# A layer's results turned by VectorE instead of TensorE, with row sums taken from the weighted product

## The chip, the cores and the metric

The kernel runs on one core of a Trainium2 chip. The metric is the device time of one execution in microseconds; lower is better. All data is float32. The engines are called PE (TensorE, the matrix engine), DVE (VectorE), ACT (ScalarE), POOL (GpSimd) and SP (SyncE, which here issues every DMA).

## What is computed

The input x has 4 batches of 128 channels and 64 x 64 = 4096 positions. Two layers follow one another:

```
# layer 0, on GroupNorm(x): q, k of 64 channels, v and gate of 128 (sigmoid)
attn = softmax(q^T k / 8);  x = x + Wp (gate * (v attn^T)) * sp + bp
# layer 1, on tokens t (4096 x 128): h = LayerNorm(t), q = h W
t = t + softmax(q q^T) h                  # same q on both sides: scores are symmetric
# feed-forward part: Wx = LayerNorm(t) W^T, batch norm over all tokens, then
y_s = sigmoid(Wx_s + y_(s-1) V^T)         # a scan over the 4096 tokens
t = t + y
```

## The kernel before

**Layers and blocks.** `fast()` does the work; `general()` is a fallback that runs only where a check of the denominators or of the scan fails. Each batch goes through `layer0` and `layer1`. Queries are taken in blocks of 512 (`QB`; `NB` = 8 blocks, `NQ` = 4 tiles of 128 in a block). All matrices on PE are float32, so a product of 512 columns is two PE instructions.

**Layer 0** (`attention`) walks 16 steps per block: two score products, one Exp over 1024 columns (L233), a running sum `acc` of the exponentials on DVE (L240) and the weighted products (L426) two steps later. `finish` of layer 0 multiplies by the gate, projects, and brings x and the projection from channels-by-tokens to tokens-by-channels with `move`: DVE turns 32 x 32 blocks into a tile `d` (L269), SP writes `d` to a scratch tensor `turn_d` in DRAM (L274), and four reads (L276) bring the blocks to the right partitions. It then keeps the tokens `t` in DRAM (`t_d`), writes the normed tokens `h` and moves a turned copy of `h` to `qt`.

**Layer 1** uses the symmetry: it takes query blocks in the order 6, 7, 5, 4, 3, 2, 1, 0 and for block n only the key blocks a = n, n-1, ..., 0. A step is half a key block: two score products (L695), the Exp (L701) and, two steps later, the `direct` products with `h` (L562). For a < n the exponentials are also turned: DVE turns 32 x 32 blocks into `dd` (L706), 16 SBUF-to-SBUF DMAs of 64 KB bring them into place in `tt` (L735), and some four steps later `reversed_products` (L575) adds block n's share to block a. `quarter` fills the diagonal block's second half from the first. Results gather in `oacc`, channels by tokens (L589, L591).

**The denominators** are sums of exponentials. The Exp instructions leave them with an accumulator output in `slots` (one Exp per 512 columns, each followed by a read of the accumulator); for the turned part DVE adds up `tt` (L580). `count` watches how many shares a block has.

**Finishing a block** (`finish` of layer 1). When a block has all its shares, small jobs join the queue `pending`: `tokens` (four PE turns of `oacc` into one PSUM bank, L631; scaling and residual, L633; LayerNorm), `result` (four PE turns of the new tokens `t1`, L644, a copy on ACT, a store to `t2_d`), two empty places, `turn` (four PE turns of the normed tokens `h2`, L653, a copy to `th`) and `inputs` (one product, L658, batch-norm statistics L659, a copy L662/L665 and a store). After each step of attention one job leaves `pending`. An empty place (`nothing`), or a step with `pending` empty, takes a job from `ahead` instead: the next batch's preparation (`prepare`), with query/key products (L354, emptied by L358, L362 and L366), values (L374, then L379, L383, L384) and gates (L389, then L390, L393).

**PSUM.** `ps_s` holds two score tiles of two banks, `ps_o` three banks for `o` and `ot`, and `ps_m` a single bank for everything else: the turns and products of `finish`, `queries` (L520) and the preparation.

**What sets the order.** The code above gives the order in which instructions are recorded. A scheduler then places them engine by engine, and each engine runs its own queue in order: an instruction that waits holds up all behind it on that engine. SP's queue is in order too.

**The end.** After the last block of the last batch (`b == B - 1 and n == 0`), whose key blocks are taken in the order 1, 0, the scan starts: 44 steps of two halves, which need the `inputs` of every block. t2 is read back from `t2_d` and y added to it before the output is stored.

Of the kernel before, what the change touches and what calls it, by code (L numbers as in the profile page):

```python
# [49 lines left out]
def conv_attn_hybrid_kernel(  # L50
# [17 lines left out]
    turn_d = [dram.tile([P, 4, NQ, 32], F32, name=f"turn{i}_d") for i in range(8)]  # L68
# [60 lines left out]
    def scales():  # L129

        nc.vector.tensor_mul(w_v, w_v, bc[:, 0, :])
        nc.vector.tensor_mul(w_p, w_p, bc[:, 2, :])

        nc.vector.tensor_scalar(par2, par[:, SG : BG + 1], 0.5, None, ALU.mult)
# [31 lines left out]
def fast(  # L166
# [13 lines left out]
    with ExitStack() as st:  # L180
# [82 lines left out]
        def move(blocks, dst):  # L263

            nonlocal n_moves
            d = work.tile([P, 4, NQ, 32], F32, tag="d", name="d", bufs=2)
            turned = nc.vector.transpose(d.rearrange("q a j i -> q j a i"), blocks)  # L269
            if n_moves == 0:  # L270
                tc.keep_in_program_order(turned)
            via = turn_d[n_moves % len(turn_d)]
            n_moves += 1
            nc.sync.dma_start(via, d)  # L274
            for a in range(4):
                nc.sync.dma_start(dst[bass.ts(a, 32)], via[:, a].rearrange("(p i) j k -> i p j k", p=4))  # L276
# [18 lines left out]
        def tiles(t):  # L295

            return [t[:, :, j, :] for j in range(NQ)]

# [112 lines left out]
        def layer0(b, gate, q, k, v, need):  # L411
# [20 lines left out]
            def finish(n, o, acc):  # L432
# [12 lines left out]
                sub = stat.tile([P, NQ, 4], F32, tag="sub", name="sub", bufs=2)  # L445

                def sums():


                    half, blocks = acc[:, 0, :], acc[:, 1, :]  # L450
                    nc.vector.tensor_tensor(half, half, blocks, ALU.add)
                    nc.vector.transpose(blocks, half)
                    nc.vector.tensor_reduce(
                        sub, blocks.rearrange("q (j f k) -> q j f k", j=NQ, f=4), AX.X, ALU.add
                    )
                    move(xb.rearrange("c (j f k) -> c j f k", j=NQ, f=4), t)

                def denominators():
                    m0, m1 = halves(quart, sub.rearrange("q j f -> q (j f)"))
                    tot = stat.tile([P, NQ, 4], F32, tag="tot", name="tot", bufs=2)  # L460
                    flat = tot.rearrange("q j f -> q (j f)")
                    nc.vector.tensor_copy(flat, m0)
                    nc.vector.tensor_tensor(flat, flat, m1, ALU.add)
                    nc.vector.tensor_tensor(
                        tot, tot,
                        own.rearrange("q (j f) -> q j f", j=1).to_broadcast([P, NQ, 4]), ALU.mult,
                    )
                    den = den_all[:, b * NT + n * NQ : b * NT + (n + 1) * NQ]
                    nc.vector.tensor_reduce(den, tot, AX.X, ALU.add)
                    nc.vector.reciprocal(rinv, den)  # L470

                def projection():
                    m0, m1 = halves(wt["ps"], og)
                    nc.scalar.copy(og, m1)
                    nc.vector.tensor_tensor(og, m0, og, ALU.add)
                    move(og.rearrange("c (j f k) -> c j f k", j=NQ, f=4), yt)

                def tokens():
                    for j in range(NQ):
                        nc.vector.scalar_tensor_tensor(  # L480
                            t[:, :, j, :], yt[:, :, j, :], rinv[:, j : j + 1], t[:, :, j, :],
                            ALU.mult, ALU.add,
                        )
                    nc.sync.dma_start(t_d[b, n], t)
                    layernorm(tiles(t), quarters(h[:, ts, :]))

                    move(
                        h[:, ts, :].rearrange("q j (p i) -> q j p i", p=4),
                        qt[:, cs].rearrange("c (p j k) -> c p j k", j=NQ, p=4),
                    )  # L490
                    done.add((b, n))
# [6 lines left out]
        def layer1(b, h, qt):  # L498
# [7 lines left out]

            slots = accp.tile([P, NT, NB + 1], F32, tag="slots", name="slots", bufs=2)
            nc.gpsimd.memset(slots[:, :, NB:], 0.0)
# [14 lines left out]
            def quarter(n, ps, e, before, slots):  # L523
# [14 lines left out]
                for half in range(2):  # L538
                    at = NQ * n + 2 + half
                    nc.scalar.activation(  # L540
                        e[:, half, hb:], ps[:, 0, bass.ts(half, hb)], AF.Exp, bias=shift,
                        accum_out=slots[:, at, n : n + 1],
                    )
                for half in range(2):
                    at = NQ * n + 2 + half
                    nc.scalar.activation(
                        e[:, half, :hb], ps[:, 1, bass.ts(half, hb)], AF.Identity,
                        accum_out=slots[:, at, NB : NB + 1],
                    )

            def order(n):


                return [1, 0] if b == B - 1 and n == 0 else list(range(n, -1, -1))
# [15 lines left out]
            def reversed_products():  # L570
# [3 lines left out]
                for j in range(NQ):  # L574
# [5 lines left out]
                nc.vector.tensor_reduce(  # L580
                    slots[:, bass.ts(n, NQ), a], t.rearrange("q p b k j -> q b p (k j)"),
                    AX.XY, ALU.add,
                )
                part(a, ot)
                count(n)

            def part(n, o):
                if n in begun:
                    nc.vector.tensor_tensor(oacc[:, n, :], oacc[:, n, :], o, ALU.add)  # L589
                else:  # L590
                    nc.vector.tensor_copy(oacc[:, n, :], o)  # L591
                begun.add(n)
                count(n)

            def count(n):


                parts[n] += 1
                if parts[n] == NB - (b == B - 1 and n == 0):
                    finish(n)  # L600

            def finish(n):
                cs = bass.ts(n, QB)
                rinv = stat.tile([P, NQ], F32, tag="rinv", name="rinv")
                t = work.tile([P, 4, NQ, 32], F32, tag="t", name="t1", bufs=2)
                if b == B - 1 and n == 0:
# [3 lines left out]
                    th, t2 = two[:, 0, :], two[:, 1, :]  # L610
# [3 lines left out]
                else:  # L614
# [3 lines left out]
                    t2 = None  # L618
# [5 lines left out]
                def tokens():  # L624
                    at = (B + b) * NT + n * NQ
                    den = den_all[:, at : at + NQ]
                    nc.vector.tensor_reduce(den, slots[:, bass.ts(n, NQ), :], AX.X, ALU.add)
                    nc.vector.reciprocal(rinv, den)
                    m = bank().rearrange("q (j c) -> q j c", j=NQ)
                    for j in range(NQ):  # L630
                        nc.tensor.transpose(m[:, j, :], oacc[:, n, bass.ts(j, P)], ident)  # L631
                    for j in range(NQ):
# [7 lines left out]
                def result():  # L640
                    nonlocal t2
                    m = bank()
                    for j in range(NQ):
                        nc.tensor.transpose(m[:, bass.ts(j, P)], t1[:, j, :], ident)  # L644
                    if t2 is None:
                        t2 = work.tile([P, QB], F32, tag="xb", name="t2")
                    nc.scalar.copy(t2, m)
                    nc.sync.dma_start(t2_d[b, :, cs], t2)

                def turn():  # L650
# [3 lines left out]
                    nc.scalar.copy(th, m)  # L654

                def inputs():
                    m = bank()
                    nc.tensor.matmul(m, lhsT=wt["f"], rhs=th, start=True, stop=True)  # L658
                    nc.vector.bn_stats(bn_st[:, b * NB + n, :], m)  # L659
                    m = m.rearrange("p (g i s) -> p i g s", i=L // 2, s=2)  # L660
                    if b == B - 1:
                        nc.vector.tensor_copy(wxs[:, :, b, bass.ts(n, GB), :], m)  # L662
                    else:
                        wx = work.tile([P, L // 2, GB, 2], F32, tag="wx", name="wx")
                        nc.vector.tensor_copy(wx, m)  # L665
                        nc.sync.dma_start(wxs_d[b, :, :, bass.ts(n, GB), :], wx)

                if b == B - 1 and n == 0:
                    pending.appendleft(tokens)
                    pending.extend([result, turn, inputs])  # L670
                elif b == B - 1 and n < 4:
                    pending.extend([tokens, result, turn, inputs])
                else:
                    pending.extend([tokens, result, nothing, nothing, turn, inputs])


            for n in [NB - 2, NB - 1] + list(range(NB - 3, -1, -1)):
# [4 lines left out]
                for a in order(n):  # L682
# [4 lines left out]
                    for i in range(2):  # L687
                        ps = ps_s.tile([P, 2, QB], F32, tag="s", name="ps")
                        e = ep.tile([P, 2, QB], F32, tag="e", name="e")
                        if a == n and i == 1:  # L690
                            quarter(n, ps, e, before, slots)
                        else:
                            for half in range(2):
# [4 lines left out]
                                )  # L698
                            for half in range(2):
                                at = NQ * a + 2 * i + half  # L700
                                nc.scalar.activation(  # L701
                                    e[:, half, :], ps[:, half, :], AF.Exp, bias=shift,
                                    accum_out=slots[:, at, n : n + 1],
                                )
# [19 lines left out]
                        if a > n and i == 1:  # L724
                            count(a)
# [571 lines left out]
```

## Time and profile before

The median of three runs is 3062.62 us (3060.75 to 3062.82). One profiled execution took 3064.04 us, with a span of 3062.2 us and a mean granted PE clock of 0.992.

| What | Busy us or count |
|---|---|
| ACT, Exp of layer 0, L233 x512 | 520.8 |
| ACT, Exp of layer 1, L701 x516, and its accumulator reads | 350.0 and 101.3 |
| DVE, running sum of layer 0, L240 x448 | 547.3 |
| DVE, turns of exponentials, L706 x444 | 287.1 |
| PE turns of `finish`, L631, L644, L653, each x124 in the main form | 19.9, 18.9, 21.1 |
| POOL, bias added to x, L443 x32 | 61.7 |
| DMA, `tt<-dd` | 1776 issues of 64 KB, 2.0 us to landing |
| DMA, moves: writes of 256 KB, reads of 64 KB | 96 and 3 x 128 issues, about 2.0 us to landing |

Busy time counts overlapping PE instructions by their union, so the duration of one says less than the distance from its start to the next one's. In a row of a group, the figures after the bar are the busy time, the mean duration of one in ns, and the engine's idle time just before with what ended it.

### The profile page before, as it was taken

The page shows a single profiled execution, that of the slowest core. Times are in us where ns is not written, and L with a number is a line of the kernel's source. Part 1 is how long each engine was busy: PE and PEld are TensorE (multiplying, and loading weights), DVE is VectorE, ACT ScalarE, POOL GpSimd, SP SyncE. Part 2 cuts the span into 40 slices and gives each one's busy share as a digit, 9 for nine tenths or more (in the row PEclk, how much of TensorE's full clock was granted, in tenths as well). Part 3 has the DMA queues.
Part 4 walks back from the last instruction along what each step waited for, and adds up shares of the span by engine and source line. Part 5 has one row for each costly group of instructions (what it writes and reads, how often), then busy time and mean ns, then how long its engine had stood idle before and what let it go on. Part 6 is the DMA issues. An engine that isn't in the chain of part 4 may idle for free.

```text
span 3062.2 us, 32664 instructions
## 1 busy us (share of the span) xinstructions
PE 3006.4 (98%) x10844; PEld 1382.7 (45%) x10844; DVE 1880.9 (61%) x3160; ACT 1151.9 (38%) x2147; POOL 149.0 (5%) x187
## 2 busy tenths in 40 slices
PE   8999999999999999999999999999999999999996
PEld 4444444444444444444444444444444444444443
DVE  6666665655666666555566666665566666455556
ACT  3443433333344443333344443333334444323334
POOL 0000000000000000000000000000000000000000
PEclk9999999999999999999999999999999999999998
DMA  1111143433111123333311113333321112543334
GB/s 42 38 56 56 49 112 87 99 89 97 48 56 56 47 80 94 92 97 91 82 47 61 42 49 110 89 96 95 93 59 57 41 50 93 138 102 93 100 104 166
DMA packets 233746, 241.16 MB, mean 79 GB/s; under 512 B 88544, under 2 KB 144352, under 8 KB 232544
## 3 DMA queue, kind: packets, MB, share of 16 engines
q1 hardware_dynamic: 233568, 238.97, 28.0%
q8 instruction: 89, 1.46, 0.2%
q14 instruction: 89, 0.73, 0.1%
HBM read 65.80 MB, written 56.62 MB: 40 GB/s over the span
## 4 chain that ended last, share of the span: by engine, by line
PE 95%; DVE 3%; issue 1%; ACT 1%; POOL 0%; DVEq 0%; POOLq 0%
PE o L426 29%; PE o L562 16%; PE ps L231 15%; PE ps L695 14%; PE ot L575 12%; PE m L260 1%; PE m L658 1%; PE mq L520 1%; PE ps L528 1%; PE mp L389 1%; PE mp L354 1%; PE mp L374 1%; DVE t2s L881 1%; DVE ps_r L854 1%; PE m L653 1%
## 5 line engine op out<-in xcount | busy, mean ns | idle before, releaser
L426 PE MATMUL o<-e,nxt 64*128 64x512 f32 x4096 | 966.2, 589 | 0.0
L233 ACT ACTIVATE e<-ps 128x1024 f32<-128x1024 f32 x512 | 520.8, 1023 | 685.2 <-PE ps L231 669.7
L240 DVE TENSOR_TENSOR acc<-acc,e 128x1024 f32<-128x1024 f32 x448 | 547.3, 1222 | 236.5 <-ACT e L233 220.8
L426 PEld LDWEIGHTS o<-e,nxt 64*128 64x128 f32 x4096 | 400.1, 187 | 483.0 <-issue 474.2
L701 ACT ACTIVATE e<-ps,shift 128x512 f32<-128x512 f32 x516 | 350.0, 683 | 675.0 <-PE ps L695 510.8
L562 PE MATMUL o<-e,h 128*128 128x512 f32 x1160 | 539.5, 592 | 0.0
L231 PE MATMUL ps<-nxt 64*128 64x512 f32 x2048 | 535.3, 596 | 1.2 <-DVE nxt L366 0.9
L695 PE MATMUL ps<-qt 128*128 128x512 f32 x1032 | 490.9, 595 | 2.9 <-ACT qt L521 2.7
L575 PE MATMUL ot<-tt,h 128*128 128x512 f32 x888 | 399.6, 593 | 0.2 <-DMA tt<-dd 0.2
L706 DVE STREAM_TRANSPOSE dd<-e 128x512 f32<-128x512 f32 x444 | 287.1, 687 | 85.9 <-ACT e L701 75.4
L562 PEld LDWEIGHTS o<-e,h 128*128 128x128 f32 x1160 | 218.2, 190 | 265.8 <-issue 261.2
L231 PEld LDWEIGHTS ps<-nxt 64*128 64x128 f32 x2048 | 194.2, 187 | 228.9 <-issue 151.3
L695 PEld LDWEIGHTS ps<-qt 128*128 128x128 f32 x1032 | 187.9, 190 | 213.5 <-issue 188.7
L575 PEld LDWEIGHTS ot<-tt,h 128*128 128x128 f32 x888 | 167.9, 190 | 210.4 <-issue 207.5
L580 DVE TENSOR_REDUCE slots<-tt 128x4 f32<-128x2048 f32 x111 | 250.8, 2259 | 9.3 <-DMA tt<-dd 8.9
L589 DVE TENSOR_TENSOR oacc<-oacc,ot 128x512 f32<-128x512 f32 x87 | 59.6, 685 | 188.3 <-PE ot L575 188.2
L138 POOL TENSOR_SCALAR rstd<-mv 128x4 f32<-128x4 f32 x64 | 14.5, 227 | 2349.7 <-DVE mv L287 2349.7
L701 ACT ACTIVATION_READ_ACCUMULATOR e<-ps,shift 128x1 f32 x516 | 101.3, 196 | 0.0
L443 POOL TENSOR_SCALAR xb<-xb,bpc 128x512 f32<-128x512 f32 x32 | 61.7, 1929 | 389.1 <-DMA xb<-in_x_dram 372.0
L480 DVE SCALAR_TENSOR_TENSOR t<-yt,rinv,t 128x128 f32<-128x128 f32 x128 | 36.5, 347 | 71.4 <-DMA yt<-turn_d 66.3
L139 POOL TENSOR_TENSOR rstd<-rstd,mhalf 128x4 f32<-128x4 f32 x64 | 66.4, 1037 | 5.3
L290 DVE TENSOR_SCALAR h<-t,mv,rstd 128x128 f32<-128x128 f32 x128 | 35.7, 342 | 47.1 <-POOL rstd L139 47.1
(161 smaller groups left out, 1667.3 us busy)
## 6 DMA issues: line engine op xcount, KB each, us to landing
tt<-dd SPq DMA_DIRECT2D x1776, 64.0 KB, 2.0
turn_d<-d SPq DMA_DIRECT2D x96, 256.0 KB, 2.0
t_d<-t SPq DMA_DIRECT2D x63, 256.0 KB, 2.0
xb<-in_x_dram SPq DMA_DIRECT2D x32, 256.0 KB, 2.9
t<-turn_d SPq DMA_DIRECT2D x128, 64.0 KB, 2.0
yt<-turn_d SPq DMA_DIRECT2D x128, 64.0 KB, 2.0
qt<-turn_d SPq DMA_DIRECT2D x128, 64.0 KB, 2.1
t<-t_d SPq DMA_DIRECT2D x32, 256.0 KB, 3.1
```

The costliest lines, as they stand in the source:

```text
L139: nc.gpsimd.tensor_tensor(dst, dst, mhalf[:, :n], ALU.pow)
L231: nc.tensor.matmul(ps[:, h, :], lhsT=lhsT, rhs=rhs, start=True, stop=True)
L233: nc.scalar.activation(e, ps, AF.Exp, scale=scale)
L240: nc.vector.tensor_tensor(acc, acc, e, ALU.add)
L426: nc.tensor.matmul(o[r], lhsT=v[rs, p + h * PAIRS, :], rhs=e[rs, h, :], start=(p == 0 and h == 0), stop=(p == PAIRS - 1 and h == 1),)
L443: nc.gpsimd.tensor_scalar(xb, xb, bpc, None, ALU.add)
L562: nc.tensor.matmul(o, lhsT=h[:, NQ * a + 2 * i + half, :], rhs=e[:, half, :], start=(a == order(n)[0] and i == 0 and half == 0), stop=(a = ...
L575: nc.tensor.matmul(ot, lhsT=h[:, NQ * n + j, :], rhs=t[:, :, j, :, :].rearrange("q p k j -> q k p j"), start=(j == 0), stop=(j == NQ - 1),)
L580: nc.vector.tensor_reduce(slots[:, bass.ts(n, NQ), a], t.rearrange("q p b k j -> q b p (k j)"), AX.XY, ALU.add,)
L695: nc.tensor.matmul(ps[:, half, :], lhsT=qt[:, bass.ts(at, P)], rhs=qt[:, bass.ts(n, QB)], start=True, stop=True,)
L701: nc.scalar.activation(e[:, half, :], ps[:, half, :], AF.Exp, bias=shift, accum_out=slots[:, at, n : n + 1],)
L706: nc.vector.transpose(d.rearrange("q f b k j -> q k b f j")[:, 2 * i + half], e[:, half, :].rearrange("q (b f j) -> q b f j", b=NQ, f=NQ),)
```

## The change

The change does four things.

1. **Row sums from the product.** After `h` has been moved to `qt`, POOL adds 1 to it. As the channels of a normed token sum to zero, the channel sum of the weighted product is then 128 times the denominator. `slots`, the accumulator outputs, the reduction of `tt` and `count` go; one Exp covers 1024 columns in layer 1 as well. The product now gives the attention output plus 1, so 1 is taken from the bias added to x (`bpc`), which a LayerNorm doesn't notice.
2. **The result turned by DVE.** `result` no longer uses PE and ACT: `turn_out` turns the tokens on DVE and writes them to `t2_d` with four scattered DMAs.
3. **Blocks 4 to 7 of layer 1 wholly without PE turns.** `finish_moved` brings `oacc` to tokens with a `move`, scales and norms, brings the normed tokens back with a second `move`, and stores the result with `turn_out`. Its jobs are spread over nine places.
4. **The move the other way round.** Where it wrote once and read four times, it now writes four times, each to its place in DRAM, and reads once. The tiles of tokens are laid out accordingly.

A block now counts as finished when its products are there, and the last block takes its key blocks as 0, 1.

```diff
+        def turn_out(blocks, dst):
             d = work.tile([P, 4, NQ, 32], F32, tag="d", name="d", bufs=2)
             turned = nc.vector.transpose(d.rearrange("q a j i -> q j a i"), blocks)
...
+            for f in range(4):
+                nc.sync.dma_start(
+                    dst.rearrange("(a i) m -> i a m", a=4)[:, :, bass.ts(f, P)],
+                    d[bass.ts(f, 32)].rearrange("i a j k -> i a (j k)"),
+                )
...
-            nc.sync.dma_start(via, d)
-            for a in range(4):
-                nc.sync.dma_start(dst[bass.ts(a, 32)], via[:, a].rearrange("(p i) j k -> i p j k", p=4))
+            turn_out(blocks, via)
+            nc.sync.dma_start(dst, via)
...
+                    hn = h[:, ts, :].rearrange("q j c -> q (j c)")
+                    nc.gpsimd.tensor_scalar(hn, hn, 1.0, None, ALU.add)
...
-                nc.vector.tensor_reduce(
-                    slots[:, bass.ts(n, NQ), a], t.rearrange("q p b k j -> q b p (k j)"),
-                    AX.XY, ALU.add,
-                )
...
+            def finish_moved(n):
...
+                def sums():
+                    ot = work.tile([P, 4, NQ, 32], F32, tag="og", name="otk")
+                    move(oacc[:, n, :].rearrange("c (j f k) -> c j f k", j=NQ, f=4), flat(ot))
+                def tokens():
+                    reciprocals(n, ot.rearrange("q p j i -> q j p i"), AX.XY, rinv)
...
+                    layernorm(tiles(t), tiles(h2))
+                    th = work.tile([P, QB], F32, tag="th", name="thm")
+                    move(h2.rearrange("q p j i -> q j p i"), th)
+                    turn_out(t.rearrange("q p j i -> q j p i"), t2_d[b, :, cs])
+                def inputs():
+                    recurrence_inputs(n, th, ps_m.tile([P, QB], F32, tag="m", name="mw"))
+                gap = [nothing] * 3
+                pending.extend([sums, *gap, tokens, *gap, inputs])
+
+            def reciprocals(n, o, axes, rinv):
+                at = (B + b) * NT + n * NQ
+                den = den_all[:, at : at + NQ]
+                nc.vector.tensor_reduce(den, o, axes, ALU.add)
+                nc.vector.tensor_scalar(den, den, 1.0 / C, None, ALU.mult)
+                nc.vector.reciprocal(rinv, den)
...
             def finish(n):
+                if n >= 4:
+                    return finish_moved(n)
...
                 def result():
-                    m = bank()
-                    for j in range(NQ):
-                        nc.tensor.transpose(m[:, bass.ts(j, P)], t1[:, j, :], ident)
-                    nc.scalar.copy(t2, m)
-                    nc.sync.dma_start(t2_d[b, :, cs], t2)
+                    turn_out(t1.rearrange("q j (p i) -> q j p i", p=4), t2_d[b, :, cs])
...
-                elif b == B - 1 and n < 4:
-                    pending.extend([tokens, result, turn, inputs])
+                elif b == B - 1 and n < 4:
+                    pending.extend([tokens, turn, inputs])
                 else:
-                    pending.extend([tokens, result, nothing, nothing, turn, inputs])
+                    pending.extend([tokens, nothing, nothing, nothing, turn, inputs])
...
-                            for half in range(2):
-                                nc.scalar.activation(
-                                    e[:, half, :], ps[:, half, :], AF.Exp, bias=shift,
-                                    accum_out=slots[:, at, n : n + 1],
-                                )
+                            nc.scalar.activation(e, ps, AF.Exp, bias=shift)
```

## The prediction

> **What bounds the kernel now.** I read the page first (busy times and the chain that ended last).
>
> ```profile
> PE 3006.4 (98%) x10844; PEld 1382.7 (45%) x10844; DVE 1880.9 (61%) x3160; ACT 1151.9 (38%) x2147; POOL 149.0 (5%) x187
> PE 95%; DVE 3%; issue 1%; ACT 1%; POOL 0%; DVEq 0%; POOLq 0%
> L580 DVE TENSOR_REDUCE slots<-tt 128x4 f32<-128x2048 f32 x111 | 250.8, 2259 | 9.3 <-DMA tt<-dd 8.9
> ```
>
> TensorE carries 95% of the chain. VectorE has 39% free, so the 250.8 us of its L580, which the change removes, are worth nothing by themselves. Next, who made TensorE wait (columns: total us, times, longest):
>
> ```profile
> PE ps L695 <- ACT qt L521: 2.7, 4, 0.7
> PE mp L354 <- DVE nxt L366: 2.5, 3, 0.8
> PE ot L575 <- DMA tt<-dd: 0.2, 1, 0.2
> ```
>
> So between the load at the head and the scan, the in-order TensorE queue is full: every instruction taken off it counts, and so does every wait put on it. What a turn costs there, from the groups by shape and the TensorE timeline:
>
> ```profile
> L644 PE MATMUL m<-ident,t1b 128*128 128x128 f32 x124 | 18.9, 275 | 0.0
> L631 PE MATMUL m<-ident,oacc 128*128 128x128 f32 x124 | 19.9, 275 | 0.0
> ...
> 2923.22 0.60 PE L644 MATMUL m<-ident,t1b 128*128 128x128 f32 x4
> 2923.66 1.03 PE L528 MATMUL ps<-qt 128*128 128x256 f32 x4
> ```
>
> A turn lasts 275 ns, but four of them give way to the next instruction after 2923.66 - 2923.22 = 0.44 us, or 0.11 us each. By starts, a 128x512 product (two instructions) takes 0.86 us. Then how long the one PSUM bank of `ps_m` stays taken by a query/key product (timelines of TensorE and VectorE):
>
> ```profile
> 537.10 1.02 PE L354 MATMUL mp<-nxt,w 128*128 128x512 f32 x2
> 537.96 1.88 PE L695 MATMUL ps<-qt 128*128 128x512 f32 x4
> ...
> 538.16 0.80 DVE L358 TENSOR_SCALAR nxt<-mp,par 64x512 f32<-64x512 f32 x1 [4.71 <-PE mp L354]
> 539.80 0.82 DVE L366 TENSOR_SCALAR nxt<-mp,par 64x512 f32<-64x512 f32 x1 [0.84 <-ACT nxt L362]
> ```
>
> TensorE is done at 537.96 and the bank is free at 540.62: 2.6 us, filled here by other products. Last, the DMA queue in block 7 and the end of layer 1:
>
> ```profile
> 518.70 22.05 SPq L735 DMA_DIRECT2D tt<-dd  x32
> 543.21 24.07 SPq L735 DMA_DIRECT2D tt<-dd  x32
> ...
> 2957.85 3.60 PE L562 MATMUL o<-e,h 128*128 128x512 f32 x8
> 2961.29 0.60 PE L644 MATMUL m<-ident,t1b 128*128 128x128 f32 x4
> 2963.55 0.66 PE L631 MATMUL ml<-ident,oacc 128*128 128x128 f32 x4 [1.66 <-DVE oacc L589]
> 2965.37 2.08 PE L658 MATMUL m<-th,w 128*128 128x512 f32 x2
> 2975.60 4.33 PE L831 MATMUL ps_r<-wxs,ident 128*128 128x256 f32 x12 [1.47 <-DVE wxs L662]
> ```
>
> SyncE needs 0.65 to 0.75 us for each `tt` issue, nearly without a pause: a second tight resource. At the end, 14.3 us pass from the last product (2961.29) to the scan (2975.60), and after the idle stretch the same product takes 2.08 us where it took 1.02 before.
>
> [...]
>
> **The change part by part.** *Turns off TensorE.* Each of the 16 finishes of blocks 4 to 7 loses 12 turns, each of the other 16 loses 4 (the result): 256 turns, 64 groups of 0.44 us. The two result groups at the end (blocks 1 and 0 of the last batch) lie beside a wait: 62 x 0.44 = **-27.3 us**.
>
> *Row sums.* Adding 1 to `h` lets the channel sum of the weighted product give the denominators. Away go L580, 516 accumulator reads (196 ns each) and half of the Exp instructions. VectorE gains some 250 us and ScalarE 130, but neither ends a wait of TensorE worth over 3 us: **0**. The added `h`+1 on GpSimd (some 1.93 us, as L443) is queued before the next `xb` and LayerNorm on an engine 5% busy: 0.
>
> *Moves.* A move was one write and four reads and is now four writes and one read: five issues either way, 0.43 us for a scattered one, 0.34 for a whole one. The wait for the landing stays. Layer 0: 0, at most 1 us later per block.
>
> *Added moves and VectorE turns.* A finish of blocks 4 to 7 now puts 16 transfers on SyncE where there were 3: 12 x 0.43 for scattered writes plus two reads and a landing wait less the old store, about 7 us, and three VectorE turns of 0.71 us. What is queued behind: the `tt` transfers, for which reversed products wait. I compared each pair's last landing with its product in the trace: 3 to 14 us to spare in batches 0 to 2, 0.2 at worst in the last, and 6 to 12 where the moves fall; the new order sets the reversed products up to 10 us later. Hidden: **0**, at most +6 in the last batch.
>
> *The order of TensorE's queue.* The scheduler placed the next batch's preparation (`ahead`) anew. I walked both built programs' TensorE order with 0.86 us per product and 0.11 per turn, and listed where a user of the `ps_m` bank follows the one before sooner than that one is emptied. In the kernel before, this gives three places of weight, 1.72 us after an L354 each; the trace has just these: 2.5 us in 3 times. The changed order has, in each of batches 0 to 2:
>
> ```
> 775 L636 mw<-thm x1
> 776 L725 ps<-qt x2
> 777 L385 mp x4
> 778 L725 ps<-qt x1
> 779 L365 mp<-nxt,w x2
> 780 L385 mp<-w,nxt x4
> 781 L577 ot<-tt,h x4
> ...
> 813 L400 mp<-nxt,w x3
> ...
> 853 L636 mw<-thm,w x1
> 854 L672 m<-ident,oacc x4
> ```
>
> (L365, L385, L400, L636 are the former L354, L374, L389, L658.) At 779 and 780 nothing stands between: two waits of 2.6 us. At 813 two waits for ScalarE, 0.78 (L390) + 0.2 = 1.0 us each. At 854 the wait for statistics and copy, 0.70 + 0.67 + 0.1 = 1.45. A like place in the next layer 0, 0.6. Sum 9.3 per batch, times 3 = **+27.9 us**; the last batch, without preparation, +0.6. Behind the waiting instruction stand all products, and nothing can catch up.
>
> *The clock.* Around 779 to 781 TensorE works 0.86 us in some 6, and at the end of the trace before, 1.66 us of idleness among short turns was enough to double the time of a product. If it halves here, [...] **+6** (0 to 9).
>
> *The end.* Block 0's denominators now come after its turns: a reduction of 0.69, two small operations of 0.2 and a VectorE turn of 0.65 join the chain, +1.7 for block 1 and again for block 0; but block 1 starts sooner. From the last product I work out 15.3 to 16.4 us against 14.3: **+1.5**.
>
> Sum: 3062.6 - 27.3 + 27.9 + 0.6 + 6 + 1.5 = **3071 us**.
>
> **The rivals.** (a) *Clean gain*: the bank's waits don't occur, because the queue is then behind for other reasons or the emptying is quicker: 3062.6 - 27.3 + 1.5 = 3037. For: the turns surely go. Against: the same walk named the three waits of the kernel before. (b) *Cancelled*: the clock doesn't dip (-6) and the gates' waits are hidden (-6): 3071 - 12 = 3059.[...] (c) *DMA queue bound*: on top of mine, SyncE's 7 us come through in part; where half of it does in the tight blocks 7 (4 of 16 finishes), 4 x 3.5 = 14: 3085. For: SyncE is near full in block 7. Against: the slack named above.
>
> **How the numbers follow.** My case 0.52 (3066 to 3076, four fifths of it slower by over 0.2%), (b) 0.23, (a) 0.12, (c) 0.13. Above 3068.7: 0.42 + 0.13 and a little of (b) = 0.58; within 0.2% (3056.5 to 3068.7): 0.29; faster 0.13. The range takes in (b) and (c) up to their middles, with the clock from 0 to 9: 3055 to 3084.
>
> **What would show it.** TensorE's waits should list `mp` L365 and L385 for VectorE L377 with about 5 us per batch, L400 for ScalarE with 2, `m` L672 for VectorE with 1.5 to 2, and 256 fewer TensorE instructions; the granted clock should dip three times, at the start of block 5. A wait list as short as before makes (a) right; long waits of `ot` L577 for `tt` make (c) right.

## The result

The changed kernel takes 3088.86 us (median of four runs, 3086.51 to 3091.43), against 3062.72 us before (median of four runs, one more than above): ratio 1.0085, 95% interval 1.0067 to 1.0102. It is 26.1 us slower. The forecast was 3071 us, slower by 8.3, with a range up to 3084: the direction was right, the time lies above the range.

### The profile page after: what moved, and what is told of

It is laid out like the page before. It is cut to its first block, busy times and chain, and to the rows that moved or that the text cites. A ratio compares the mean times of both kernels' runs of the same rounds, so it can differ in the third digit from the quotient of the medians.

```text
span 3087.9 us, 31588 instructions
## 1 busy us (share of the span) xinstructions
PE 2991.4 (97%) x10588; PEld 1365.9 (44%) x10588; DVE 1698.4 (55%) x3146; ACT 1022.5 (33%) x1133; POOL 222.5 (7%) x215
## 4 chain that ended last, share of the span: by engine, by line
PE 88%; SPq 5%; DVE 4%; DMA 1%; issue 1%; ACT 1%; POOL 0%; DVEq 0%
PE o L437 29%; PE ps L233 15%; PE o L564 14%; PE ps L725 12%; PE ot L577 11%; SPq L759 5%; PE m L262 1%; PE mq L529 1%; PE mp L365 1%; PE mp L385 1%; PE mp L400 1%; PE ps L537 1%; DVE t2s L905 1%; DVE ps_r L878 1%; DMA tt<-dd 1%
## 5 line engine op out<-in xcount | busy, mean ns | idle before, releaser
L729 ACT ACTIVATE e<-ps,shift 128x1024 f32<-128x1024 f32 x258 | 287.1, 1113 | 801.6 <-PE ps L725 435.8
L233 PE MATMUL ps<-nxt 64*128 64x512 f32 x2048 | 545.8, 595 | 2.0 <-DVE nxt L377 0.9
L725 PE MATMUL ps<-qt 128*128 128x512 f32 x1032 | 483.8, 594 | 2.7 <-ACT qt L530 2.7
L577 PE MATMUL ot<-tt,h 128*128 128x512 f32 x888 | 411.4, 607 | 11.0 <-DMA tt<-dd 7.0
L732 DVE STREAM_TRANSPOSE dd<-e 128x512 f32<-128x512 f32 x444 | 278.1, 679 | 148.5 <-DMA tt<-dd 93.8
L577 PEld LDWEIGHTS ot<-tt,h 128*128 128x128 f32 x888 | 171.5, 195 | 227.7 <-issue 222.8
L502 POOL TENSOR_SCALAR h<-h 128x512 f32<-128x512 f32 x32 | 72.3, 2260 | 63.7 <-DVE d L270 59.6
L588 DVE COPY oacc<-ot 128x512 f32<-128x512 f32 x24 | 16.6, 692 | 86.7 <-PE ot L577 86.6
```

The source lines that it names most:

```text
L233: nc.tensor.matmul(ps[:, h, :], lhsT=lhsT, rhs=rhs, start=True, stop=True)
L502: nc.gpsimd.tensor_scalar(hn, hn, 1.0, None, ALU.add)
L577: nc.tensor.matmul(ot, lhsT=h[:, NQ * n + j, :], rhs=t[:, :, j, :, :].rearrange("q p k j -> q k p j"), start=(j == 0), stop=(j == NQ - 1),)
L725: nc.tensor.matmul(ps[:, half, :], lhsT=qt[:, bass.ts(at, P)], rhs=qt[:, bass.ts(n, QB)], start=True, stop=True,)
L729: nc.scalar.activation(e, ps, AF.Exp, bias=shift)
L732: nc.vector.transpose(d.rearrange("q f b k j -> q k b f j")[:, 2 * i + half], e[:, half, :].rearrange("q (b f j) -> q b f j", b=NQ, f=NQ),)
```

## The profile after

The page of the changed kernel gives these busy times and this chain of work that ended last:

```profile
PE 2991.4 (97%) x10588; PEld 1365.9 (44%) x10588; DVE 1698.4 (55%) x3146; ACT 1022.5 (33%) x1133; POOL 222.5 (7%) x215
PE 88%; SPq 5%; DVE 4%; DMA 1%; issue 1%; ACT 1%; POOL 0%; DVEq 0%
```

The 256 instructions are gone from PE, and VectorE and ScalarE are relieved as the change meant it. But the chain, which before was PE for 95% and had no share of SyncE's queue (SPq), is PE for 88% and the queue for 5%. The list of who made TensorE wait (total us, times, longest) has the names:

```profile
PE mp L365 <- DVE nxt L377: 9.4, 5, 2.6
PE mp L385 <- DVE nxt L377: 7.7, 3, 2.6
PE ot L577 <- DMA tt<-dd: 7.0, 4, 3.0
PE ml L688 <- DVE last L298: 6.9, 1, 6.9
...
PE m L672 <- DVE wx L643: 5.1, 6, 1.4
PE mp L400 <- ACT nxt L401: 4.3, 5, 0.9
...
PE ot L577 <- issue: 4.0, 4, 2.5
```

The lines of `mp` and of `m` L672 are the waits for the `ps_m` bank that the forecast named, at its places; 2.5 us of them, ahead of three L365, were there before. The two lines of `ot` L577, 11.0 us together, are new: before, `ot` waited for `tt` 0.2 us once. Next comes the first place where the preparation's products stand together, at the start of block 5 in batch 0, first in TensorE's timeline and then in windows of 3.41 us (first the length, then PE's busy time; the third figure from the right is the granted clock):

```profile
558.77 1.12 PE L365 MATMUL mp<-nxt,w 128*128 128x512 f32 x2 [2.56 <-DVE nxt L377]
562.45 2.08 PE L385 MATMUL mp<-w,nxt 128*128 128x128 f32 x8 [2.56 <-DVE nxt L377]
564.32 5.39 PE L577 MATMUL ot<-tt,h 128*128 128x512 f32 x8
```

```profile
557.68:561.09 3.41, 1.12 (x2) 0.30 (x2) 1.62 (x2) 0.50 (x2) 0.00 (x0) 1.00 0.35 57
561.09:564.51 3.42, 2.06 (x9) 2.06 (x10) 0.82 (x1) 0.45 (x1) 0.00 (x0) 0.50 0.00 0
564.51:567.92 3.41, 3.41 (x6) 1.34 (x5) 3.35 (x6) 1.92 (x3) 0.00 (x0) 0.50 0.00 0
567.92:571.33 3.41, 3.41 (x10) 1.50 (x9) 1.62 (x4) 0.94 (x1) 0.00 (x0) 1.00 0.31 77
```

TensorE waits 2.56 us twice, and then the granted clock is 0.50 for 6.83 us: eight instructions of L577, begun at half clock, take 5.39 us. What such a stretch of half clock, a dip, costs is shown best by two places that are alike, behind the `inputs` of a moved block (one that `finish_moved` finishes) in batches 0 and 1:

```profile
730.56 0.65 PE L672 MATMUL m<-ident,oacc 128*128 128x128 f32 x4 [1.38 <-DVE wx L643]
732.52 6.68 PE L577 MATMUL ot<-tt,h 128*128 128x512 f32 x8 [1.30 <-DMA tt<-dd]
...
1472.04 0.65 PE L672 MATMUL m<-ident,oacc 128*128 128x128 f32 x4 [1.38 <-DVE wx L643]
1473.84 3.67 PE L577 MATMUL ot<-tt,h 128*128 128x512 f32 x8 [1.15 <-DMA tt<-dd]
```

The waits are nearly the same. In batch 0 the clock falls (731.76 to 738.59) and eight instructions take 6.68 us; in batch 1 it doesn't, and they take 3.67. The next table goes by stage: layer 1 of a batch with the layer 0 that follows it, and layer 1 of the last batch.

| Stage | before, us | after, us | PE waits before, after | at half clock, after |
|---|---|---|---|---|
| batch 0 | 733.1 | 742.1 | 1.7, 11.7 | 13.7 |
| batch 1 | 733.0 | 739.3 | 1.7, 12.2 | 6.8 |
| batch 2 | 733.0 | 743.4 | 1.7, 14.0 | 10.2 |
| batch 3, layer 1 | 384.7 | 384.6 | 7.9, 15.5 | 12.7 (before 10.7) |

Between the end of the last product of attention (2984.5) and the scan 16.2 us pass, where 15.3 to 16.4 had been worked out:

```profile
2995.20 1.24 PE L688 MATMUL ml<-ident,last 128*128 128x128 f32 x4 [6.86 <-DVE last L298]
...
3000.66 2.90 PE L855 MATMUL ps_r<-wxs,ident 128*128 128x256 f32 x6 [1.47 <-DVE wxs L640]
```

Last, this is SyncE's queue in the last batch while a block is finished with moves:

```profile
2784.69 0.58 SPq L600 DMA_DIRECT2D t<-t_d  x1
2785.32 1.89 SPq L274 DMA_DIRECT2D turn_d<-d  x4
...
2789.28 0.44 SPq L284 DMA_DIRECT2D otk<-turn_d  x1
2790.07 8.11 SPq L759 DMA_DIRECT2D tt<-dd  x13
2800.37 1.78 SPq L274 DMA_DIRECT2D turn_d<-d  x4
2802.25 1.38 SPq L274 DMA_DIRECT2D t_d<-d  x3
2803.81 0.34 SPq L284 DMA_DIRECT2D thm<-turn_d  x1
2804.19 0.44 SPq L274 DMA_DIRECT2D t_d<-d  x1
```

Issuing takes 0.58 + 1.89 + 0.44 + 1.78 + 1.38 + 0.34 + 0.44 = 6.9 us, as forecast (7). The pauses, such as 2.2 us ahead of 2800.37 for VectorE's tile `d`, come on top: some 10 us for a block. For a pair, that is a query block with an earlier key block, the 16 `tt` transfers take 10.05 us back to back, 0.63 us each.

## The experiments

The theory after this reading is that three costs add up: the waits for the `ps_m` bank, the waits for `tt` because SyncE's queue is full, and the half clock that follows both. Its rivals are the moves themselves, the row sums, or an accident of order. The kernel before took 3063.5 to 3063.7 us beside these runs; ratios are against it.

### The preparation's order alone

```diff
-                nc.tensor.matmul(m, lhsT=wt["qk"], rhs=xg[:, cs], start=True, stop=True)
+                tc.keep_in_program_order(nc.tensor.matmul(m, lhsT=wt["qk"], rhs=xg[:, cs], start=True, stop=True))
```

The same is done for L385 and L400. A product so pinned keeps its recorded place behind what was recorded before it.

> The changed kernel with the preparation's products (L365, L385, L400) pinned behind what is recorded before them, so that the scheduler can't draw them together. Walked by hand, its TensorE order has none of the waits for VectorE and ScalarE inside the preparation. Theory (three costs add up: waits for the one ps_m bank, half clock after them, waits for tt): the bank waits go, 3 x 9.1 = 27 us, and the three half-clock windows at the start of block 5 of 6.83 us with them, 3 x 3.4 = 10 us; the waits for tt (11 us) and their windows stay: 3052. Rival 1 (the DMA queue takes it back): a TensorE that is some 10 us earlier per batch meets SyncE where it has no time to spare; the tt waits grow by 10 to 20 us: 3062 to 3075. Rival 2 (the order matters little, the loss comes from the moves themselves): over 3080.

Measured: 3051.61 us, ratio 0.9964 (0.9950 to 0.9979). The work is the same, only the order differs, and 37.3 us are gone against the changed kernel. All waits of `mp` are gone from the list, and so are the three dips at the start of block 5. The waits for `tt` stay:

```profile
PE ot L577 <- DMA tt<-dd: 10.2, 7, 2.6
...
PE ot L577 <- issue: 3.0, 3, 2.5
```

So the order costs 37 us, and the change without it would have won 12 us. The first rival fell: the queue took back only about 2 us (13.2 against 11.0). The sum came out as worked out, but not each part: where three dips had followed waits for `tt`, the pinned kernel has one, of 3.41 us; its mean granted clock is 0.992, where the changed kernel has 0.987.

### The finishing DMAs on GpSimd's queue

```diff
-        def move(blocks, dst):
+        def move(blocks, dst, q=nc.sync):
...
-            turn_out(blocks, via)
-            nc.sync.dma_start(dst, via)
+            turn_out(blocks, via, q)
+            q.dma_start(dst, via)
```

`turn_out` issues its four writes on `q`, too, and `finish_moved` passes `nc.gpsimd` for both moves and the result.

> The changed kernel with the DMAs of finish_moved (two moves and the scattered store, 14 per block) issued by GpSimd instead of SyncE; what is computed is the same. The scheduler's order of TensorE changes with it: walked by hand it keeps of the bank waits only 0.98 at L365 and 0.64 at L672 per batch. Theory: bank waits, tt waits and half clock all go, 3088.9 - 25 - 10 - 11 - 6 = 3037. If the tt waits come from something else than SyncE's queue (the two dd tiles, the transfers themselves), they stay: about 3052, as for the pinned kernel. Rival (GpSimd's queue is slower, and its waits for landings delay rstd of the LayerNorms): th comes late and inputs wait, over 3060.

Measured: 3034.10 us, ratio 0.9905 (0.9888 to 0.9921). No wait of `ot` is left in the list, and the clock is full from 23 to 2931 us (mean granted clock 0.992, where the changed kernel has 0.987). Had the transfers themselves or the two `dd` tiles been the cause, the waits should have stayed. But the scheduler's order changed here too, so the two causes are not yet apart.

### Without the moves of blocks 4 to 7

```diff
-                if n >= 4:
+                if n >= NB:
                     return finish_moved(n)
```

> The changed kernel with finish_moved left out: blocks 4 to 7 finish as blocks 0 to 3 do, with TensorE turns of oacc and h2 and the result by turn_out. Theory: 32 groups of turns come back (32 x 0.44 = 14 us), the walked order has bank waits of 5.0 us in all where the kernel before has 2.5 to 3, SyncE has only three issues per block more than before: 3062.6 - 31 x 0.44 + 2 = 3051, 38 us below the changed kernel, with a clock that doesn't dip before the end. Rival (row sums or the move the other way round cost the time): it stays near 3075 to 3085.

Measured: 3050.99 us, ratio 0.9959 (0.9945 to 0.9973), as worked out, though two errors nearly cancel in that: the row sums cost more than nothing and the turns of the result bring more, as the next two kernels show. The result's turn by VectorE is a gain by itself; the loss came in with the moved blocks and the order that the scheduler made with them. The kernel with the queue on GpSimd does without 32 more groups of turns and is 16.9 us faster: 0.53 each, with all else that differs between the two.

### Row sums and the other move alone

The former `result` with its turns, its copy and its store stands again, besides the edit above; what is left of the change is the row sums, the move the other way round, and the new rule for when a block is finished. In the first of these two kernels the copy leaves the columns of a block of the result in another order; in the second it puts them in place.

> Of the change only the row sums from the product and the move the other way round: finish_moved is left out and the result is again turned on TensorE, copied by ScalarE and stored whole. TensorE has as many turns as before. Theory (VectorE and ScalarE are off the path, a move costs the same either way): 3062 within 3. Rival (the relief of VectorE frees TensorE from waits, or the finish that waits for the product costs at the end): 3055 or 3070.

> Of the change only the row sums from the product and the move the other way round, as the earlier run of that kind, in which the copy of the result left the columns of a block in another order; here ScalarE's copy puts them in place. Theory: the same time as that run, 3066.9, since only a copy's access pattern differs; it says whether the row sums are worth 0 as forecast or cost some 3 us. Rival: the strided copy lengthens the hold of the bank, 3068 to 3072.

Measured: 3066.87 us and 3067.33 us, ratios 1.0010 and 1.0011 (both 1.0004 to 1.0017). So these parts together cost 3.5 us, not 0; which of them does is not shown. By the page of the first, VectorE is busy 1665.2 us instead of 1880.9 and ScalarE 1050.7 instead of 1151.9, and none of it comes back. The first of the two kernels has a new wait:

```profile
PE m L687 <- DVE t1b L676: 1.6, 3, 0.5
```

It stands against 2.2 us of waits of the former L653 for VectorE's `h`, of which 0.7 are left. So these waits (1.6 and 0.7 us against 2.2) don't explain the 3.5 us; where they went stays open. The kernel without the moves of blocks 4 to 7 does without 32 groups of turns more than these two and is 16.1 us faster, 0.50 each, again with all else that differs.

### Which of the moves' DMAs fill SyncE

Both edits are made in the pinned kernel: first only the two reads of a moved block go to GpSimd, then only the twelve writes. In the diff, `w` is the queue of the writes and `r` that of the reads.

```diff
-        def move(blocks, dst):
+        def move(blocks, dst, w=nc.sync, r=nc.sync):
...
+            turn_out(blocks, via, w)
+            r.dma_start(dst, via)
```

> The pinned kernel, in which only the two whole reads of a moved block (otk and thm) are issued by GpSimd; the twelve scattered writes stay on SyncE. In the changed kernel SyncE spends 6.9 us of issuing on a moved block and some 3.2 us waiting for landings and for VectorE's turned tile. Theory A (issue time: SyncE's capacity in the last batch is what lacks): 6.1 of 6.9 us stay, most of the tt waits stay: 3045 to 3050. Theory B (the reads' waits for a landing hold up the tt transfers behind them): the waits for tt go, 3035 to 3038.

> The pinned kernel, in which only the twelve scattered writes of a moved block are issued by GpSimd; the two reads stay on SyncE and wait there for GpSimd's writes to land. Theory A (issue time): 5.2 of 6.9 us are gone from SyncE, the waits for tt nearly vanish: 3034 to 3039. Theory B (the reads' waits): they stay and grow a little, since the writes land later: 3048 to 3060.

Measured: 3046.14 us (ratio 0.9942, 0.9926 to 0.9959) without the reads, 3038.19 us (0.9915, 0.9899 to 0.9932) without the writes. Both fit theory A: the time that the writes take on SyncE weighs more than the reads' waiting. The reads, which take 0.8 of the 6.9 us of issuing, still gave 5.5 us, so their waits have a share. And with the writes SyncE also loses its waits for VectorE's tile `d`, as the 2.2 us above; issuing and those waits are not told apart here. With the writes on GpSimd no wait of `ot` for `tt` is left, but the product of a moved block's `inputs` now waits for its read:

```profile
PE mw L636 <- DMA thm<-turn_d: 2.6, 3, 1.9
```

### Both remedies

The edits of the first two experiments stand together.

> Both remedies at once: the preparation's products pinned, and all fourteen finishing DMAs of a moved block on GpSimd. Walked by hand its bank waits are 3.5 us in all, against 5.7 in the kernel with the DMAs on GpSimd alone. Theory (the gain of that kernel is the sum of the two losses undone, not a third thing that its other order brings): the same within 3 us, 3032 to 3037. Rival (part of its gain is an accident of its order): 3040 or more.

Measured: 3028.46 us, ratio 0.9884 (0.9868 to 0.9901). With the preparation pinned in both, taking the DMAs off SyncE is worth 3051.6 - 3028.5 = 23.1 us. Most of it has a name in the traces: 13.2 us are the waits of `ot`, 5.7 the turns of L688 that wait for VectorE (11.1 us pinned, 5.4 here), and 1.7 half of the dip's 3.41. Only the preparation is pinned, though: in order of start, 1283 of TensorE's 10,588 places hold another instruction, so for the last 2.5 us the order is not ruled out. The rival fell, but the theory's number was missed as well: this kernel is 5.6 us better than the queue alone. 2.8 us of it are waits of TensorE that are no more (0.95 per batch); where the rest went stays open.

### More blocks moved

This is the kernel with the finishing DMAs on GpSimd, with all eight blocks of batches 0 to 2 moved:

```diff
-                if n >= 4:
+                if n >= 4 or b < B - 1:
```

> The kernel with the finishing DMAs on GpSimd, and all eight blocks of batches 0 to 2 finished by finish_moved (in the last batch blocks 4 to 7 as before). 12 more finishes lose two groups of turns: 24 x 0.44 to 0.49 = 10.6 to 11.8 us. If TensorE's queue still has no other wait: 3034.1 - 11 = 3023. Rival (late moves at the end of a batch, where four or five blocks finish close together, make inputs wait or hold up VectorE's turns): 3030 to 3040.

Measured: 3038.86 us, ratio 0.9916 (0.9900 to 0.9933). The gain did not come, as the rival has it: the kernel is 4.8 us slower than with four blocks moved. The waits lie at the start of layer 0, as the list for TensorE and the timelines of VectorE and ScalarE show:

```profile
PE ps L233 <- ACT e L235: 16.9, 7, 4.2
```

```profile
846.64 0.69 DVE L631 TENSOR_REDUCE den_all<-otk 128x4 f32<-128x512 f32 x1 [7.25 <-DMA otk<-turn_d]
```

```profile
848.56 1.02 ACT L235 ACTIVATE e<-ps 128x1024 f32<-128x1024 f32 x1 [5.80 <-DVE den_all L632]
855.59 1.02 ACT L235 ACTIVATE e<-ps 128x1024 f32<-128x1024 f32 x1 [6.00 <-DVE acc L242]
```

The reduction waits 7.25 us for a move, and VectorE's running sum `acc` stands behind it (847.25 to 848.46), so the Exp at 848.56 comes late. Then VectorE does the block's tokens before the next `acc` (854.31), and the Exp waits another 6.00 us; the scores wait for the Exp. VectorE has time free on average (it is busy for 55% of the changed kernel's span), but what is due first stood behind a wait of 7.25 us. Hence the last kernel, with blocks 2 to 7 moved in batches 0 to 2:

```diff
-                if n >= 4:
+                if n >= (2 if b < B - 1 else 4):
```

> The kernel with the finishing DMAs on GpSimd, in batches 0 to 2 with blocks 2 to 7 finished by finish_moved and blocks 0 and 1 by TensorE turns (last batch as before: 4 to 7). Six more finishes lose two groups of turns of 0.49: -5.9. Theory (with all eight moved, block 0's and 1's moves at the start of layer 0 held up VectorE's running sum; without those two it has no such wait): 3034.1 - 5.9 = 3028. Rival (already the third and fourth block crowd GpSimd's queue): 3034 or more.

Measured: 3022.11 us, ratio 0.9863 (0.9846 to 0.9879): 41.6 us faster than the kernel before and 66.7 faster than the changed one. The waits of layer 0 are gone. It is 12.0 us better than with four blocks, where 5.9 were worked out: 2.1 are waits (0.7 per batch); where the rest went stays open, as above.

## Why the prediction was wrong

**The step that failed is "Hidden: 0, at most +6 in the last batch"** for the moves on SyncE. Its 7 us of issuing were right. But they were held against the time to spare of one pair at a time in the trace before (6 to 12 us), as if each finish met a queue that had recovered. The forecast also took 0.65 to 0.75 us for a `tt` issue from two stretches with pauses in them; back to back it is 0.63, so the queue was less full than it seemed, and still had too little left.

What happened is plainest in the last batch. From the end of the issues of one pair (2784.7) to those of the twelfth after it (2937.4), SyncE pauses only where the moves make it wait, some 2 us at a time: 152.7 us, of which twelve pairs take 12 x 10.05 = 121 and three moved blocks the other 32. TensorE does the twelve pairs in 149.8 us. Before, it had 154.5 us, and the three finishes took SyncE about 1 us each, so some 31 us were free there:

```profile
2770.04 0.33 SPq L648 DMA_DIRECT2D t_d<-t  x1
2770.48 43.41 SPq L735 DMA_DIRECT2D tt<-dd  x64
2813.94 0.58 SPq L622 DMA_DIRECT2D t<-t_d  x1
```

What TensorE leaves the queue per pair, 12.5 - 10.05 = 2.4 us, takes more than four pairs to make up for one moved block, and there are four to five pairs between two. The time to spare is 7.0 us at the first pair of block 5; then TensorE waits for one pair each in blocks 5, 4 and 3 (2.46, 0.32 and 0.55 us).

The larger part of the cost lies in batches 0 to 2, where the forecast had 0, and the same sum gives it. In batch 0, between two pairs of block 3, SyncE waits 2.9 us for VectorE's tile `d` and then issues a block's moves:

```profile
705.31 8.11 SPq L759 DMA_DIRECT2D tt<-dd  x13
716.39 1.78 SPq L274 DMA_DIRECT2D turn_d<-d  x4
...
720.70 20.37 SPq L759 DMA_DIRECT2D tt<-dd  x32
```

From 647.4, the end of the issues of block 5's last pair, to 730.9, the end of those of the pair that TensorE then waits for, SyncE needs 83.5 us: six pairs take 60, and two moved blocks with one store the other 23. TensorE needs 78.6 us for these pairs and had 3.8 us to spare at the first, so 1.1 us are missing; it waited 1.30.

The reversed products waited 11.0 us in all (6.1 in batches 0 to 2, 4.9 in the last), and three further dips followed these waits; the 3.41 us ahead of the one in batch 0 held 1.38 us of waiting for the bank as well. The granted clock in a dip is 0.50, so as an estimate half of what a dip leaves after its own idle time is lost: the three cost (6.83 - 0.76 + 3.41 + 3.41 - 0.15) / 2 = 6.4 us. Together that is 17.4 us: 10.9 in batches 0 to 2 against 0 forecast, and 6.5 in the last batch against "at most +6". This is the rival (c), given 3085 and a chance of 0.13. Its 14 us came near 17.4, but by luck: it expected the waits in block 7, and of the eight waits four were in block 3, two in block 4, and one each in blocks 5 and 7.

**The bank waits** were right in place and size: 6 x 2.56 (L365, L385) + 6 x 0.87 (L400) + 3 x 1.38 + 3 x 0.32 (L672) = 25.7 us, against 27.9. **The clock** at block 5 dipped three times as forecast, and each dip lasted 6.83 us. Part of that was idle: (3 x 6.83 - 1.36 - 2.56 - 1.42) / 2 = 7.6 us, by the same estimate, against 6. The forecast's 6 was an estimate that no trace had shown. Clean gain (a) and cancelled (b) fell with these two, as rivals for this kernel. The pinned kernel with GpSimd's queue comes to 3028 where (a) had 3037, but because its order and its queue are others, not for (a)'s reasons.

**The turns** were taken too low: 0.44 us a group from one place in the trace, where the two pairs of runs give 0.50 and 0.53, so 33.0 us instead of 27.3. **The row sums** and the move the other way round were costed at nothing and cost 3.5 together. **The end** was right: 16.2 us against 14.3 before is +1.9, where +1.5 was forecast.

The sum by these figures is -33.0 + 3.5 + 25.7 + 7.6 + 17.4 + 1.9 = +23.1 against +26.1 measured; where the other 3 us went stays open. The errors in the turns and the row sums (-2.2 together) hardly moved the result; SyncE's queue did.

## What to carry to other kernels

Where a queue has a steady load, a burst added to it must be held against what it makes up per step, not against the time to spare at one step: divide the burst, with the waits inside it, by the surplus per step and compare with the distance to the next burst (here some 10 us by 2.4 us per pair, with four to five pairs between two bursts). When a scheduler is free to place side work, look at its order for users of a single PSUM bank drawn together: pinning three lines was worth 37 us here, more than the two kernels differ by. And an engine with much idle time can still hold up everything, when an instruction that waits for a DMA stands in its queue ahead of a steady chain, as VectorE's reduction did for 7.25 us with eight moved blocks.

## What the runs showed of the hardware

**Half clock inside attention.** Between 30 us and the end of the last product of attention (2984.5, before 2961.3), the trace of the changed kernel has six dips, and the trace before has none. In the next table, waiting is the length of a stretch less PE's busy time in it.

| Dip from, us | lasts, us | waiting in the 3.41 us ahead, us | waiting in its first 3.41 us |
|---|---|---|---|
| 561.09 | 6.83 | 2.29 | 1.36 |
| 731.76 | 6.83 | 1.92 | 0.76 |
| 1301.79 | 6.83 | 2.54 | 2.56 |
| 2042.48 | 6.83 | 2.29 | 1.42 |
| 2216.56 | 3.41 | 3.02 | 0.00 |
| 2837.78 | 3.41 | 2.31 | 0.15 |

The starts and ends lie multiples of 3.41 us apart. If the stretch from 30 to 2984.5 us is divided into pieces of 3.41 us from there, none of the other pieces at full clock holds more than 1.47 us of waiting. In the pinned kernel 3.41 us with 1.73 us of waiting (2796.16 to 2799.57) are followed by full clock. The two waits that are nearly alike in batches 0 and 1, above, fall differently on this division: they put 1.92 us into one piece and 0.76 into the next in batch 0, where the clock falls, and 1.38 and 1.15 in batch 1, where it doesn't. How much waiting brings a dip is not shown beyond these numbers.

**Half clock at the end.** In the trace before, the clock falls at 2964.88, and the 3.41 us ahead hold 1.67 us of waiting (2961.47 to 2964.88), nearly all of it the 1.66 us that the prediction names. The pinned kernel kept its clock with 1.73, so waiting alone doesn't tell. The other 1.74 us of the 3.41 are turns alone; whether that makes the difference, no run here tests.
